# A perceiver block with routed experts on one core: one load moved up the queue, one projection moved between scores, second expert layers moved behind the next first half

## The chip, the cores and the metric

The kernel runs on one core of one Trainium2 chip. A core has TensorE (PE, matrix products; its weight loads are shown apart as PEld), VectorE (DVE), ScalarE (ACT), GpSimd (POOL) and SyncE (SP, which here only issues DMAs), each with its own in-order list of instructions. The metric is the device time of one execution in microseconds (us), as a median over runs. Everything is computed in float32.

## What is computed

The reference, cut to what matters. `x` is 64 sequences of 32 tokens of 256; `ctx_512` is 64 contexts of 257 rows of 128.

```python
x = x + xattn(layernorm(x), ctx_512)   # 16 heads of 64; q from x, k and v from the context; softmax over 257 rows
x = x + attn(layernorm(x))             # 4 heads of 64 over the 32 tokens of a sequence, half of each head rotated
x = x + ffn(layernorm(x))              # mixture of 8 experts, each token to its best 2

# ffn, for all 2048 tokens
scores = x @ Wr.T + br
idx    = top_k(scores + biases_N, 2);  val = softmax(scores) at idx, scaled to sum 1
h      = x @ Wl1[n] + bl1[n]           # 256 -> 1024, split in halves a and b
y      = sum over the two experts n of val[n] * ((silu(a) * b) @ Wl2[n] + bl2[n])   # 512 -> 256
```

## The kernel before

**Tiles and sequences.** The 2048 tokens are 16 tiles `t` of 128 tokens, that is 4 sequences `b` each. One loop over the 64 pairs (t, b) does the cross attention of a sequence and, between its pieces, other tiles' work. Two sequences overlap: while (t, b) is transposed and mixed, the scores of the next pair are made. `cross_probs` (L359) is a generator of four pieces: a score product `s` (L369), its negated maximum `nmx` on DVE (L373), the exponential `pr` on ACT with its sum (L374), and after each second one the scaling on DVE (L379, L381). The `s` tiles have three PSUM banks, so the fourth score of a sequence needs the bank of the first, which ACT's exponential frees. `probs_transposed` (L389) transposes the probabilities (`tp`, L392), `cross_mix` (L399) multiplies them with the context (`pa`, L402).

**What is done in between.** `work` holds three generators: "near" and "far" are `rest(t)` (L597) of the last finished tile and of the one before it, and "ahead" makes queries of later tiles. `rest` is `cross_output` (output projection `po`, L431 and L435), `self_attention` (transposes `trs`; the projection `pqkv`, L450, 2 products of 512 and 2 of 256 columns; `trqk`; scores `pss`; `pot`; output `apo`) and `route` (transposes `trr`, scores `pr`, ranks `pk`, two scatters of the rows to `routed` in memory, L578, then `pw` and `pb`). Each `next` does one piece. Which piece comes where is written by hand: the table `steps` has a row for each b of six places, and `step()` (L945) takes the next. Even and odd tiles use the same four rows. The row for b == 3 is

```python
        ("near", "far", "ahead", "", "far", "far"),
```

whose first "near" is the tile's `pqkv` group, standing ahead of the first two scores of the next pair. In odd tiles "ahead" is at its end by then.

**The 257th context row.** The loop treats 256 context rows; the last row's part is added as one product in `cross_output`, `po` <- `u`, `lastT` (L431), before the others of `po` (L435, four, a yield, four). The rows `u` are worked out once at the start, kept in memory (`u_last`), and `load_last(t)` (L296) fetches a tile's 64 rows with four DMAs into one of three buffers, at b == 3 of the tile.

**The experts.** Tokens are gathered from `routed` in blocks of 128 rows for one expert. Six early blocks are taken from what the tiles before the last three have scattered, so that they can run among the last tiles' remains; 28 late blocks follow, with branches for more that this input doesn't take. A block has five steps, all on `Blocks` (L660 on): `gathered` (one DMA, its row number read into a register of SP), `prepared` (transposes `pxT`, copy `bxT` on ACT, gate and target rows on DVE), `first_half` (`pa`, 8 groups of a pair of products, L726), `second_half` (`pb` the same; then `silu` of `pa` on ACT, L740, and `g` = (`pb` + bias) * silu on DVE, L745, four each), and `combined` (the second layer `py` <- `g`, L757; `y` = `py` * gate on DVE, L762; an accumulating scatter to the output by POOL, L763). Weights lie in lanes, three for the late blocks and two of them for the early ones; a lane holds both layers of an expert (1028 and 512 KB) and `weights` (L683) reloads a layer once its last reader is done, and only where the expert changes.

**Queues.** SP issues its DMAs in the program's order, and each waits for its buffer, so what stands behind a waiting one waits too. The order on PE and SP is the program's; on DVE, ACT and POOL a planner sets it from the program.

**Around the change.** In the last tile (t == 15) at b == 2, SP gets the six early gathers and the weights of block 0; at b == 3 comes `load_last(15)`. The gathered rows have five buffers, one of which was taken before, and the sixth gather needs the first block's to be free again. After the loop `do(...)` (L994) runs a hand-written list of units: "near" and "far" as above, and "x", "a", "b", "c" with a block's number for `prepared`, `first_half`, `second_half` and `combined`. Then `run` (L1027) does the late blocks:

```python
            blocks.first_half(b)
            blocks.second_half(b)
            if b + LANES < hi:
                blocks.weights(b + LANES, (0,))
            if b > lo:
                blocks.combined(b - 1)
```

Of the kernel before, what the change touches and what calls it, by code (L numbers as in the profile page):

```python
# [19 lines left out]
NT = TOK // P  # L20
# [16 lines left out]
EARLY = 6  # L37
LATE = NBK - EARLY
LANES = 3
LIKELY = (34 - EARLY, 36 - EARLY)  # L40
# [10 lines left out]
def block_kernel(  # L51
# [46 lines left out]
    def load(dst, src):  # L98
        nc.sync.dma_start(out=dst, in_=src)
# [16 lines left out]
    def load_tokens(t):  # L116
        xs[t] = xrp.tile([P, D], FP, tag="x", name=f"x{t}")
        load(xs[t], x[t * P : (t + 1) * P, :])

    def load_context(t):  # L120
        kv = kvp.tile([P, W1LEN], FP, tag="kv", name=f"kv{t}")
        kvT = kv[:, : 4 * M].rearrange("p (b m) -> p b m", b=4)
        kvA = kv[:, 4 * M : 4 * M + 4 * ML].rearrange("p (b c d) -> p b c d", b=4, c=MC)
        load(kvT, ctx_t[:, 4 * t : 4 * t + 4, :])
        load(kvA, ctx_a[:, 4 * t : 4 * t + 4, :, :])
        return kvT, kvA
# [54 lines left out]
    def iota(shape, pattern, base, by_partition, name):  # L181
        it = const.tile([P] + shape, FP, name=name)
        nc.gpsimd.iota(
            it,
            pattern,
            base=base,
            channel_multiplier=by_partition,
            allow_small_or_imprecise_dtypes=True,
        )
        return it  # L190
# [4 lines left out]
    before = iota([P], [[1, P]], 0, -1, "before")  # L195
# [7 lines left out]
    late = iota([LATE], [[1, LATE]], 0, 0, "late")  # L203
# [92 lines left out]
    def load_last(t):  # L296
        for h4 in range(4):
            load(
                u_ring[t % 3][h4 * 32 : h4 * 32 + 16, :],
                u_last[h4, 16 * t : 16 * t + 16, :],  # L300
            )
# [87 lines left out]
    def probs_transposed(t, b, j, pr, pts):  # L389
        tp = ps.tile([P, 4 * P], FP, tag="t", bufs=2, name=f"tp{t}_{b}_{j}")  # L390
        for g in range(4):
            nc.tensor.transpose(  # L392
                tp[:, g * P : (g + 1) * P], pr[:, g, j * P : (j + 1) * P], ident
            )
        pt = ptp.tile([P, 4 * P], FP, tag=f"pt{j}", name=f"pt{t}_{b}_{j}")
        nc.scalar.copy(pt, tp)  # L396
        pts.append(pt)
# [251 lines left out]
    def lane_of_queries(i):  # L649
        flat = qp.tile([P, 8, XH, SEQ], FP, tag="q", name=f"lane{i}")  # L650
        flat = flat.rearrange("p a h n -> p (a h n)")
        lanes.append((flat[:, :W1LEN], flat[:, W1LEN : W1LEN + W2LEN]))
# [118 lines left out]
    def early_blocks():  # L771


        bl = Blocks("early", EARLY, lambda b: b % 2)
        count = counted("early")
        full = in_blocks(count, 0, "early")
        last = up_to(full, "early")
        wide = [P, EARLY, NE]
        blk = early.rearrange("p a (l o) -> p (a l) o", o=1)
        past, eb = over_blocks(  # L780
            ALU.is_ge, blk.to_broadcast(wide), last.to_broadcast(wide), "eb_early"
        )
        _, begin = over_blocks(ALU.mult, past, full.to_broadcast(wide), "begin_early")
        nc.vector.tensor_tensor(bl.mine, early_expert, eb.to_broadcast(wide), ALU.is_equal)
        first = small([EARLY], "first_early")
        nc.vector.tensor_tensor(first, blk[:, :, 0], begin[:, :, 0], ALU.subtract)
        nc.vector.tensor_scalar(first, first, float(P), None, ALU.mult)
        ebf = eb[:, :, 0]
        nc.vector.scalar_tensor_tensor(
            bl.meta[:, 0, :], ebf, float(CAP), first, ALU.mult, ALU.add  # L790
        )
        nc.vector.tensor_copy(bl.meta[:, 1, :], ebf)
        nc.vector.tensor_tensor(bl.meta[:, 2, 2:], ebf[:, 2:], ebf[:, :-2], ALU.not_equal)
        done = small([1, NE], "done")
        nc.vector.tensor_tensor(done, full, last, ALU.subtract)
        nc.vector.tensor_scalar(done, done, float(EARLY), 0.0, ALU.add, ALU.max)
        nc.vector.tensor_tensor(done, done, full, ALU.min)
        return bl, done

    def late_blocks(done):  # L800
# [74 lines left out]
    steps = (  # L875
        ("", "far", "ahead", "near", "far", ""),
        ("near", "far", "", "near", "far", ""),
        ("ahead", "far", "ahead", "near", "far", "ahead"),
        ("near", "far", "ahead", "", "far", "far"),
    )  # L880
    kvs, probs = {0: context0}, {}
    seqs = [(t, b) for t in range(NT) for b in range(4)]
# [3 lines left out]
    with tc.tile_pool(name="rope", bufs=1) as rp:  # L886
# [27 lines left out]
        c4 = rp.tile([P, 16], FP, name="c4")  # L914
# [3 lines left out]
        c2 = rp.tile([P, 16], FP, name="c2")  # L918
# [12 lines left out]
    for n, (t, b) in enumerate(seqs):  # L931
        if t == NT - 1 and b == 0:
            blocks, done = early_blocks()
            lane_of_queries(0)
        if b == 0:
            cT = wk.tile([P, XH, 4, SEQ], FP, tag="cT", name=f"cT{t}")
            lastT = wk.tile([P, 4, SEQ], FP, tag="lastT", name=f"lastT{t}")
            if t + 1 < NT:
                kvs[t + 1] = load_context(t + 1)
            if t % 2 == 0 and t + 4 < NT:  # L940
                for j in (t + 4, t + 5):
                    load_tokens(j)
        place = iter(steps[b])

        def step():  # L945
            name = next(place)
            if name:
                next(work[name], None)

        scores = iter(())  # L950
        if n + 1 < len(seqs):
            t1, b1 = seqs[n + 1]
            scores = cross_probs(t1, b1, kvs[t1][0])
        pr, pts = probs.pop((t, b)), []
        probs_transposed(t, b, 0, pr, pts)
        step()
        next(scores, None)
        next(scores, None)
        step()
        probs_transposed(t, b, 1, pr, pts)  # L960
        nc.vector.transpose(lastT[:, b, :], p_last[t % 2][b])
        next(scores, None)
        step()
        next(scores, None)
        step()
        step()
        cross_mix(t, b, pts, kvs[t][1], cT)
        step()
        if t == NT - 1 and b == 2:
            for i in range(EARLY):  # L970
                blocks.gathered(i)
            blocks.weights(0, (0, 1), sure=True)
        if b == 3:
            load_last(t)
            if t % 2:
                for _ in work["ahead"]:
                    pass
                if t + 3 < NT:
                    work["ahead"] = cross_queries((t + 3) // 2)
                    next(work["ahead"])  # L980
            for _ in work["far"]:
                pass
            work["far"] = work["near"]
            work["near"] = rest(t, cT, lastT, u_ring[t % 3])
# [9 lines left out]
    def do(units):  # L994
        for unit in units.split():
            if unit in work:
                next(work[unit], None)
            else:
                b = int(unit[1:])
                {  # L1000
                    "x": blocks.prepared,
                    "a": blocks.first_half,
                    "b": blocks.second_half,
                    "c": blocks.combined,
                }[unit[0]](b)
                if unit[0] == "c" and b + 2 < EARLY:
                    blocks.weights(b + 2, (0, 1))

    do("near far x0")
    blocks.gathered(EARLY - 1)  # L1010
    do("near far near a0 far near b0 near far x1 c0 near a1 near far x2 b1 far a2")
    do("near c1 near far x3 b2 far near c2 far near a3 near x4 b3")
    late, total = late_blocks(done)
    do("c3")
    for b in range(3):
        late.gathered(b)
    do("near a4 near b4 x5 c4")
    late.weights(1, (0, 1))
    do("a5 b5")
    late.prepared(0)  # L1020
    do("c5")
    late.weights(2, (0, 1))
    blocks = late

    def run(lo, hi):  # L1027
        for b in range(lo, hi):
            if b + 3 < hi:
                blocks.gathered(b + 3)  # L1030
            if b + 1 < hi:
                blocks.prepared(b + 1)
            blocks.first_half(b)
            blocks.second_half(b)
            if b + LANES < hi:
                blocks.weights(b + LANES, (0,))
            if b > lo:
                blocks.combined(b - 1)
                if b - 1 + LANES < hi:
                    blocks.weights(b - 1 + LANES, (1,))  # L1040
            if b == 4:
                yield
        blocks.combined(hi - 1)
# [8 lines left out]

    main = run(0, LIKELY[0])
    next(main)
    used = nc.values_load(  # L1057
        total[0:1, :],
# [63 lines left out]
```

## Time and profile before

| | us |
|---|---|
| median of 3 runs | 852.11 (851.6 to 853.08) |
| the profiled execution, whole | 853.89 |
| its span, first to last instruction | 851.9 |
| TensorE granted clock, mean | 0.986 |
| first wait of TensorE, at the start | 7.27 |
| the 256 exponentials on ACT, L374 | 120.8 |
| the 512 score products, L369 | 143.4 |
| the 256 mixes, L402 | 123.3 |
| POOL's 28 late scatters, L763 | 43.4 |

The profile is of one execution. A row of a timeline gives its start, its length, the engine, the line and operation, what it writes and reads, how many instructions it merges, and in brackets how long the engine was idle before it and what ended that wait. A wait view sums such idle times: total, times, longest. "SPq" rows are SP issuing a DMA; their length is the time to issue, not the transfer. "PEclk" is the clock granted to TensorE, in tenths of full speed or as a mean.

### The profile page before, as it was taken

To read this page: it belongs to the slowest core of one execution; us is meant where nothing else is said; L and a number is where in the kernel's file an instruction comes from. 1 tells how busy PE (TensorE), PEld (TensorE's weight loads), DVE (VectorE), ACT (ScalarE), POOL (GpSimd) and SP (SyncE) were. 2 spreads that over 40 slices of the span, in tenths; PEclk is the share of its full clock that TensorE was granted. 3 is DMA by queue.
4 is the path that set the end of the run, shared out by engine and by line. 5 is a ranking of instruction groups with operands and counts; after the bars stand their busy time and mean duration, and the time that the engine had idled before them with its cause. 6 is when DMAs were issued, how large, how long until landed. Compare 5 with 4: busy or idle time off the path is not lost. (4 is left out here: it accounts for less than half of the span.)

```text
span 851.9 us, 15173 instructions
## 1 busy us (share of the span) xinstructions
PE 794.0 (93%) x5240; PEld 611.9 (72%) x5240; DVE 489.2 (57%) x2006; ACT 382.3 (45%) x1082; POOL 147.4 (17%) x209
## 2 busy tenths in 40 slices
PE   4899999999999999999999999999949999999994
PEld 3567677677767766776766777666647799999993
DVE  2456656766676676667676666767626733333331
ACT  2565545455455445546554545554414332222220
POOL 5001011111101011121101011110112422322222
PEclk9999999999999999999999999999979999999997
DMA  8421102020120202021120202012061297357321
GB/s 300 125 53 53 63 1 72 1 85 19 55 75 11 74 0 86 7 67 37 49 72 2 72 1 72 20 53 55 1 258 13 69 318 216 47 110 221 52 38 22
DMA packets 32031, 62.71 MB, mean 74 GB/s; under 512 B 5256, under 2 KB 22672, under 8 KB 30416
## 3 DMA queue, kind: packets, MB, share of 16 engines
q1 hardware_dynamic: 25424, 52.65, 19.0%
q0 software_dynamic: 6528, 9.06, 6.0%
q8 instruction: 43, 0.70, 0.3%
q14 instruction: 36, 0.29, 0.1%
HBM read 83.23 MB, written 13.16 MB: 113 GB/s over the span
## 5 line engine op out<-in xcount | busy, mean ns | idle before, releaser
L374 ACT ACTIVATE pr<-s,nmx 128x257 f32<-128x257 f32 x256 | 120.8, 479 | 72.6 <-DVE nmx L373 71.4
L369 PE MATMUL s<-kv,q 128*128 128x257 f32 x512 | 143.4, 389 | 7.6 <-ACT pr L374 7.6
L373 DVE TENSOR_REDUCE nmx<-s 128x1 f32<-128x257 f32 x256 | 103.8, 420 | 61.7 <-PE s L369 59.9
L402 PE MATMUL pa<-pt,kv 128*128 128x512 f32 x256 | 123.3, 604 | 5.0 <-ACT ov L426 5.0
L369 PEld LDWEIGHTS s<-kv,q 128*128 128x128 f32 x512 | 88.8, 192 | 25.1 <-ACT pr L374 12.2
L396 ACT COPY pt<-tp 128x512 f32<-128x512 f32 x128 | 75.9, 593 | 65.2 <-PE tp L392 65.1
L392 PEld LDWEIGHTS tp<-ident,pr 128*128 128x128 f32 x512 | 60.7, 144 | 33.7 <-issue 20.9
L392 PE MATMUL tp<-ident,pr 128*128 128x128 f32 x512 | 81.4, 280 | 1.2 <-DVE pr L381 1.1
L381 DVE TENSOR_SCALAR pr<-pr,inv 128x256 f32<-128x256 f32 x256 | 80.5, 357 | 2.9
L405 ACT COPY cT<-pa 128x512 f32<-128x512 f32 x64 | 37.5, 586 | 88.7 <-PE pa L402 88.7
L578 POOL DMA_INDIRECT routed<-xr,rslots x32 | 32.8, 1025 | 250.7 <-DVE pr L381 105.4
L402 PEld LDWEIGHTS pa<-pt,kv 128*128 128x128 f32 x256 | 44.9, 190 | 40.6 <-issue 29.1
L345 PE MATMUL pqh<-xqT,xwq_sb 128*128 128x256 f32 x256 | 62.5, 389 | 4.3 <-ACT xqT L253 4.3
L763 POOL DMA_INDIRECT out_x<-y_late,to_late x28 | 43.4, 1550 | 110.3 <-DVE gate_late L705 41.4
L435 PE MATMUL po<-xwo_sb,ov 128*128 128x256 f32 x256 | 61.9, 386 | 0.0
L345 PEld LDWEIGHTS pqh<-xqT,xwq_sb 128*128 128x128 f32 x256 | 48.6, 195 | 11.6 <-ACT xqT L253 4.7
L435 PEld LDWEIGHTS po<-xwo_sb,ov 128*128 128x128 f32 x256 | 49.7, 194 | 7.1
L379 DVE RECIPROCAL inv<-sums 128x2 f32<-128x2 f32 x128 | 20.6, 161 | 55.9 <-ACT pr L374 55.2
L745 DVE SCALAR_TENSOR_TENSOR g_late<-pb_late,lane,sa_late 128x128 f32<-128x128 f32 x72 | 20.3, 343 | 55.5 <-PE pb_late L726 37.0
L374 ACT ACTIVATION_READ_ACCUMULATOR pr<-s,nmx 128x1 f32 x256 | 51.8, 203 | 0.0
L410 POOL TENSOR_TENSOR xb<-x,xbo_bc 128x256 f32<-128x256 f32 x16 | 11.6, 725 | 213.7 <-issue 198.5
L450 PE MATMUL pqkv<-awqkv_sb,xaT 128*128 128x512 f32 (+1 forms) x128 | 43.9, 486 | 0.0
(256 smaller groups left out, 1286.5 us busy)
## 6 DMA issues: line engine op xcount, KB each, us to landing
lane<-in_wall SPq DMA_DIRECT2D x24, 1028.0 KB
lane<-in_wall SPq DMA_DIRECT2D x24, 512.0 KB
lane2a<-in_wall SPq DMA_DIRECT2D x10, 1028.0 KB
kv<-in_ctx_t SPq DMA_DIRECT2D x16, 514.0 KB
kv<-in_ctx_a SPq DMA_DIRECT2D x16, 512.0 KB
lane2b<-in_wall SPq DMA_DIRECT2D x10, 512.0 KB
xg_late<-routed SPq DMA_DIRECT2D x28, 132.5 KB
x<-in_x SPq DMA_DIRECT2D x16, 128.0 KB
```

Source lines behind the costliest of these rows:

```text
L345: nc.tensor.matmul(pq[:, mm, :], xwq_sb[:, k, m * P : (m + 1) * P], xqT[:, k, :], start=(k == 0), stop=(k == 1),)
L369: nc.tensor.matmul(s, qb[:, g * P : (g + 1) * P], kvT[:, b, :], start=True, stop=True)
L373: nc.vector.tensor_reduce(nmx, s, AX.X, ALU.max, negate=True)
L374: nc.scalar.activation(pr[:, g, :], s, AF.Exp, bias=nmx, accum_out=sums[:, g : g + 1])
L381: nc.vector.tensor_scalar(pr[:, i, :ML], pr[:, i, :ML], inv[:, i : i + 1], None, ALU.mult)
L392: nc.tensor.transpose(tp[:, g * P : (g + 1) * P], pr[:, g, j * P : (j + 1) * P], ident)
L396: nc.scalar.copy(pt, tp)
L402: nc.tensor.matmul(pa, kvA[:, b, j, :], pts[j], start=(j == 0), stop=(j == MC - 1))
L405: nc.scalar.copy(cT[:, :, b, :], pa.rearrange("p (h n) -> p h n", n=SEQ))
L435: nc.tensor.matmul(po, ov[:, m, :], xwo_sb[:, m, :], start=False, stop=(m == XH // 2 - 1))
L450: nc.tensor.matmul(pq, xaT[:, k, :], awqkv_sb[:, k, lo:hi], start=(k == 0), stop=(k == 1))
L763: nc.gpsimd.indirect_dma_start(out=out[:, :], out_offset=bass.IndirectOffsetOnAxis(ap=self.to[:, b : b + 1], axis=0), in_=y, in_offset=Non ...
```

## The change

Three edits.

1. `load_last(15)` is called at b == 2 of the last tile, ahead of the early gathers and the first weights, and no longer at b == 3 behind them.
2. `steps` has eight rows, four for even and four for odd tiles. The odd ones differ in the row for b == 3 alone: its first place is empty and "near", the `pqkv` group, is the third place, between the third and the fourth score of the next pair.
3. In the list after the loop and in `run`, the second layer of a block comes after the first half of the next block, not ahead of it or behind its second half; some "near", "far" and "x" units change places with their neighbours. The last early block's second layer and the load of the weights of late block 2 move into `run`, behind the first half of late block 0 (`last_early`).

```diff
@@ steps
         ("near", "far", "ahead", "", "far", "far"),
+        ("", "far", "ahead", "near", "far", ""),
+        ("near", "far", "", "near", "far", ""),
+        ("ahead", "far", "ahead", "near", "far", "ahead"),
+        ("", "far", "near", "", "far", "far"),
     )
...
-        place = iter(steps[b])
+        place = iter(steps[4 * (t % 2) + b])
...
         if t == NT - 1 and b == 2:
+            load_last(t)
             for i in range(EARLY):
                 blocks.gathered(i)
             blocks.weights(0, (0, 1), sure=True)
         if b == 3:
-            load_last(t)
+            if t < NT - 1:
+                load_last(t)
...
     do("near far x0")
     blocks.gathered(EARLY - 1)
-    do("near far near a0 far near b0 near far x1 c0 near a1 near far x2 b1 far a2")
-    do("near c1 near far x3 b2 far near c2 far near a3 near x4 b3")
+    do("near far near a0 far x1 b0 near far near c0 near a1 near far b1 x2 far a2 near c1")
+    do("far near x3 b2 far near c2 far near a3 near x4 b3")
     late, total = late_blocks(done)
-    do("c3")
+    do("a4 c3")
     for b in range(3):
         late.gathered(b)
-    do("near a4 near b4 x5 c4")
+    do("near b4 near x5 a5 c4")
     late.weights(1, (0, 1))
-    do("a5 b5")
+    do("b5")
     late.prepared(0)
-    do("c5")
-    late.weights(2, (0, 1))
-    blocks = late
+    early_ones, blocks = blocks, late
 
-    def run(lo, hi):
+    def run(lo, hi, before=None):
         for b in range(lo, hi):
             if b + 3 < hi:
                 blocks.gathered(b + 3)
             if b + 1 < hi:
                 blocks.prepared(b + 1)
             blocks.first_half(b)
-            blocks.second_half(b)
-            if b + LANES < hi:
-                blocks.weights(b + LANES, (0,))
             if b > lo:
                 blocks.combined(b - 1)
                 if b - 1 + LANES < hi:
                     blocks.weights(b - 1 + LANES, (1,))
+            elif before:
+                before()
+            blocks.second_half(b)
+            if b + LANES < hi:
+                blocks.weights(b + LANES, (0,))
...
+    def last_early():
+        early_ones.combined(EARLY - 1)
+        late.weights(2, (0, 1))
+
-    main = run(0, LIKELY[0])
+    main = run(0, LIKELY[0], last_early)
```

## The prediction

> **What bounds the kernel now.** I read the page first (busy shares, the 40 slices), then the chain, then TensorE's waits, then around its longest wait the timelines of PE, SP's queue and POOL, and last the end of the late blocks.
>
> ```profile
> PE 794.0 (93%) x5240; PEld 611.9 (72%) x5240; DVE 489.2 (57%) x2006; ACT 382.3 (45%) x1082; POOL 147.4 (17%) x209
> ...
> PEclk9999999999999999999999999999979999999997
> ```
> TensorE bounds nearly everything, so only its idle time (58 us of 851.9) and its slow slice, the 31st, can be won.
>
> ```profile
> PE po L431 <- DMA u<-u_last: 9.7, 1, 9.7
> PE s L369 <- ACT pr L374: 7.6, 10, 1.1
> ...
> PE py_early L757 <- DVE g_early L745: 2.1, 3, 0.9
> ...
> PE trs L252 <- DVE to_early L707: 1.3, 1, 1.3
> ```
> These are the waits that the three parts of the change touch. The timelines place them: PE, SP's queue, POOL, in that order.
>
> ```profile
> 546.33 0.70 PE L369 MATMUL s<-kv,q 128*128 128x257 f32 x2 [0.76 <-ACT pr L374]
> ...
> 617.11 0.38 PE L698 MATMUL pxT_early<-ident,xg_early 128*128 128x128 f32 x2
> 627.23 1.19 PE L431 MATMUL po<-u,lastT 128*128 128x256 f32 x2 [9.74 <-DMA u<-u_last]
> 628.22 3.22 PE L435 MATMUL po<-xwo_sb,ov 128*128 128x256 f32 x8
> ```
> ```profile
> 588.33 29.54 SPq L680 DMA_DIRECT2D xg_early<-routed  x6
> 618.44 0.87 SPq L689 DMA_DIRECT2D lane<-in_wall  x2
> 619.36 0.43 SPq L595 DMA_DIRECT2D out_x<-x  x1
> 619.83 2.08 SPq L99 DMA_DIRECT2D u<-u_last  x4
> 621.96 0.65 SPq L99 DMA_DIRECT2D lane2a<-in_wall  x1
> 624.40 0.36 SPq L99 DMA_DIRECT2D lane2b<-in_wall  x1
> ```
> The sixth gather holds SP until x0's transposes (617.11) free its buffer. Behind it stand the first weights, and behind these the four u loads; so TensorE, ready at 617.49, stood until 627.23.
>
> ```profile
> 627.23 0.96 POOL L578 DMA_INDIRECT routed<-xr,rslots  x1 [5.61 <-DMA routed<-xr,rslots]
> 634.29 0.72 POOL L520 TENSOR_TENSOR axb<-x,abo_bc 128x256 f32<-128x256 f32 x1 [6.10 <-DVE x L440]
> 636.24 0.57 POOL L242 TENSOR_TENSOR rstds<-ves,minus_half 128x1 f32<-128x1 f32 x1 [1.23 <-DVE ves L240]
> ```
> POOL's second scatter of tile 13 waits for the first; tile 15's rstds stands behind it. It was covered by the stall.
>
> ```profile
> 769.97 1.12 DVE L745 SCALAR_TENSOR_TENSOR g_late<-pb_late,lane2a,sa_late 128x128 f32<-128x128 f32 x4 [3.08 <-PE pb_late L726]
> ...
> 843.16 1.55 POOL L763 DMA_INDIRECT out_x<-y_late,to_late  x1 [3.18 <-DMA out_x<-y_late,to_late]
> ```
> The late blocks run without a TensorE wait. The end hangs on the second last scatter's DMA, not on the last product.
>
> **What the skill says.** (1) "TensorE: Matmul & The Clock Gate", Part 1: an idle window of some 3.4 us halves the clock, a busy one restores it. The trace agrees: the windows view grants 0.50 from 622 to 627.2, 0.51 to 631, 1.00 after. (2) "DMA: Bandwidth & Descriptors", Anatomy of one DMA: 2.0 us plus bytes at 436 GB/s, an estimate of 4.4 us for 1028 KB. Here it was longer: lane2b's issue waited 1.7 us "<- DMA lane" until 624.35, so I read the first weights (issued 618.44) as landed then, 5.9 us. I use 5.9. (3) Same page, Issuing engines are not separate DMA queues: all run on the same 16 engines; 622 to 627.2 shows them 94% busy, so fetching u sooner does not make the weights land much sooner. (4) The first page, "Architectural detail: the array is 16× 32×32, not 1× 128×128": ACT, DVE and each GpSimd core are strict FIFO, as rstds behind the scatter shows.
>
> **Part 1, u sooner.** Its four issues (4 x about 0.46 us on SP) now stand before the gathers of 588.33, in a gap of SP (583.40+1.84 to 588.33, 3.1 us); the gathered rows are first used at 617. Free. Removed: 9.74 us of wait and the slow clock after it: L431 and the first half of L435 took 631.37-627.23=4.14 us here (the next row, pss, starts at 631.37) and 593.32-591.16=2.16 for tile 14, so 2.0. Together 11.7.
> What is late next? I count u from 617.49. TensorE now does po 2.16, pss 0.31, po's rest 1.73: at u=4.2 it wants pa_early of block 0. Its weights still follow x0 on SP and land at 624.35, u=6.9. New wait 2.6 us (1.6 to 3.2: u's 64 KB lie no longer behind it, lane2's 1540 KB come sooner). A pause this long may drop the clock once: 0 to 1.7 us (half of 3.4), I take 0.7.
> Then pa 1.79, pot 0.6, pxT 0.22, pb 1.79: u=11.3, and trs of tile 15 is due. POOL's second scatter still waits for the first one's DMA until 627.2 (u=9.7): 0.96 scatter, 0.72 axb, 0.57 rstds, 0.41 xns (DVE L245), 0.2 of hand-overs, u=12.6. New wait 1.3, in place of the old 1.30 there (0 to 2).
> Part 1 net: 11.7-2.6-0.7=8.4.
>
> **Part 2, the order up to the first late blocks.** The products are the same. Old waits in that stretch besides those above: pxT 0.77, apo 0.93, g_early 0.93+0.93+0.28, together 3.8; they go because a first half now stands ahead of each second layer (1.79 us of cover for g's 1.13) and pxT stands after pb. New ones, from the order of the changed build and the rows of before:
> - trqk of tile 15: DVE now does apo's sum, bn, xr (2.5 us) ahead of the qkv sums and rotation (2.3 us): late by 0.5.
> - pa_early of block 2: in before bxT's copy ended 650.82-645.26=5.56 us after the first half of block 1 began, behind an activation-table load of 1.28 and apr. TensorE now wants it after 1.79+0.31+0.22+1.79+0.22+0.37=4.7: late by 0.8.
> - pot then waits for diag: 0.4.
> - trr of tile 15: POOL now has a scatter (1.18) ahead of rstdr, itself behind y_early's (1.58): late by 1.3.
> - pa_early of block 5 stands right after its own pxT: copy 0.37 and two hand-overs, 0.5.
> - py_early of block 4: g's last three are strewn through DVE's chain of late_blocks, which takes 678.18-668.36=9.8 us in before; late by 0.9. No g stands between metadata and gathers more than before.
> - pa_late of block 0 after its pxT: 0.3.
> Sum 4.7 against 3.8: -0.9 (bounds +3 and -4, as each rests on a list in order of mean durations). The first late weights keep 1.3 us of cover (issue to landing 5.3 us read off the DMA traffic of 680 to 686).
>
> **Part 3, odd tiles.** In t=1, 3 .. 13 the fourth score waits for ACT: 0.84+6x0.76=5.4 us, since nothing stands between third and fourth. The two pqkv groups (2.58 us) now do. Checks: s0 starts 2.6 us sooner, its bank was free long before; the qkv sums then end 2.6+0.5 us later, 4 us ahead of trqk; pa needs pqkv's bank, which DVE frees about 0.6 us before; the next tp needs the fourth softmax's scaling, which ends within 0.2 us of need. I take 5.0 (3.3 to 5.4). Even tiles keep their rows; tile 15 has no scores left there.
>
> **Part 4, late blocks.** py(b-1) now follows pxT and pa(b), 0.22+1.79=2.01 us after pb(b-1). g starts 0.1 us after pb and takes 1.12: ready after 1.28 with a hand-over. Slack 0.73 in each block, no wait. y(b-1) (0.48) runs under pb(b). SP's two weight waits change places with what releases them. In the middle it is worth 0.
> At the end: y of block 26 comes 1.79 us sooner, so its scatter does (838.43 to 836.65) and its DMA, 843.16-838.43=4.73 later, at 841.38. The last py now waits 1.26 for its g: py ends 840.8, y 841.3, scatter 841.55. Against 843.16: 1.6 gained (0 to 1.8).
>
> **Sum.** 8.4-0.9+5.0+1.6=14.1 of 851.9: span 837.8. That execution took 853.89 whole, 1.99 around the span, so 839.8 for it; it lies 1.8 above the median of 852.11. On the median: 838.0.
>
> **Rivals.**
> - More cover (12%): weights land by u=4.2 and none of the new waits of part 2 arises: 11.7+3.8+1.3+5.4+1.6=23.8, 828. For it: each of them is my list, not a row. Against: weights and scatter are DMAs that no edit moves.
> - The stall moves (19%): clock falls, the weights come at u=7.4, part 2 loses its 4, part 3 gives 3.3: 11.7-3.2-1.7-4+3.3+0.5=6.6, 845.5. For it: the DMA engines are full from 619 to 634. It covers the case that the change brings only half of what it says.
> - No change within 0.2% (2%): pa_early waits as long as po did. Against: weights landed 2.9 us before u, and po's products come ahead.
> - Slower (4%): g not ready in the late blocks. Decides from 0.73 us beyond my 1.28; each us more costs 27, so 0.52 us of wait per block eats the 14.1 and 1 us gives 865. For it: 0.73 us is thin, and the slack is the same in all blocks, so a miss would be paid 27 times. Against: g's start 0.1 us after pb and its 1.12 us recur in every block of before, and DVE is busy 40.8 of 118 us from 720 to 838.
>
> **Numbers.** Likeliest case 63%, 832 to 843. Range 830 to 846 (the first two rivals partly left out). This kernel's measurement can tell about 0.2%, 1.7 us: faster 94%, within 2%, slower 4%.
>
> **What would show it.** Right: no PE wait on u; one of 2 to 3 us at pa_early on lane and about 1 us at trs; no s<-ACT wait of 0.76 in odd tiles; py_late with no wait but the last, about 1.2; the last scatter some 3.7 us after the last pb ends. Wrong: a py_late wait in every block, a pa_early wait over 4 us, or a clock of 0.5 for more than 4 us after 615.

## The result and the profile after

| | before | changed |
|---|---|---|
| median of 4 runs each, us | 851.86 (850.83 to 853.08) | 836.32 (835.06 to 837.68) |
| ratio | | 0.9818 [0.9804, 0.9831] |
| profiled execution, whole, us | 853.89 | 835.06 |
| its span, us | 851.9 | 833.3 |

The changed kernel takes 15.5 us less (14.4 to 16.7 by the interval). I had forecast 838.0, 14.1 less. Run again beside another series of before it took 836.74 against 851.85, ratio 0.9822 [0.9797, 0.9846].

The page of the changed kernel, TensorE's busy time and its granted clock by slices:

```profile
PE 792.6 (95%) x5240; PEld 613.0 (74%) x5240; DVE 490.1 (59%) x2006; ACT 378.5 (45%) x1080; POOL 147.2 (18%) x209
...
PEclk9999999999999999999999999999999999999998
```

TensorE is as busy as before to 1.4 us; the slow slice is gone (it is the 30th of the 40, not the 31st, as the prediction has it). So what was won is idle time and the slow clock behind it. The waits of TensorE in the changed kernel (engine, line, what it waited for, then total, times, longest in us):

```profile
PE tp L392 <- DVE pr L381: 2.0, 3, 0.8
PE pa_early L726 <- DMA lane<-in_wall: 1.9, 1, 1.9
PE s L369 <- ACT pr L374: 1.8, 2, 1.1
...
PE pa_early L726 <- ACT bxT_early L700: 1.0, 2, 0.5
...
PE trs L252 <- DVE xns L245: 0.7, 1, 0.7
PE py_late L757 <- DVE g_late L745: 0.5, 1, 0.5
PE trqk L252 <- DVE qkv L465: 0.4, 1, 0.4
PE pxT_late L698 <- DVE g_early L745: 0.4, 1, 0.4
```

No wait on `u` is left. Its place is taken by the first weights (1.9); `trs` still waits 0.7. `s` fell from 10 waits to 2, `py_early` has none, `py_late` one of 28. The timeline of PE in the same kernel shows the places:

```profile
536.70 0.60 PE L369 MATMUL s<-kv,q 128*128 128x257 f32 x2
537.14 2.74 PE L450 MATMUL pqkv<-awqkv_sb,xaT 128*128 128x512 f32 x8
539.72 0.60 PE L369 MATMUL s<-kv,q 128*128 128x257 f32 x2
...
610.11 0.38 PE L698 MATMUL pxT_early<-ident,xg_early 128*128 128x128 f32 x2
610.37 0.70 PE L431 MATMUL po<-u,lastT 128*128 128x256 f32 x2
...
616.95 2.98 PE L726 MATMUL pa_early<-bxT_early,lane 128*128 128x128 f32 x16 [1.92 <-DMA lane<-in_wall]
619.87 1.12 PE L509 MATMUL pot<-diag,qkv 128*64 128x128 f32 x8
...
623.96 0.44 PE L252 MATMUL trs<-ident,xns 128*128 128x128 f32 x2 [0.67 <-DVE xns L245]
...
645.50 0.44 PE L252 MATMUL trr<-ident,xr 128*128 128x128 f32 x2 [1.40 <-DVE xr L245]
...
821.56 1.99 PE L757 MATMUL py_late<-lane2b,g_late 128*128 128x256 f32 x8 [0.50 <-DVE g_late L745]
```

In tile 13 the projection stands between the third and the fourth score, and the fourth no longer waits. `po` on `u` follows `x0`'s transposes at once. SP's queue of the changed kernel (the length of a merged row includes the waits between its issues):

```profile
576.96 4.70 SPq L99 DMA_DIRECT2D u<-u_last  x8
582.48 28.38 SPq L680 DMA_DIRECT2D xg_early<-routed  x6
611.43 0.87 SPq L689 DMA_DIRECT2D lane<-in_wall  x2
```

The last `u` load is issued by 581.7, nearly 30 us before it is used. The sixth gather still holds SP until `x0` has read its buffer, and the weights stand behind it as before. POOL in the changed kernel, around `trs` and at the end:

```profile
613.30 1.06 POOL L578 DMA_INDIRECT routed<-xr,rslots  x1 [17.00 <-DMA xg_early<-routed]
621.22 0.96 POOL L578 DMA_INDIRECT routed<-xr,rslots  x1 [6.85 <-DMA routed<-xr,rslots]
622.20 0.74 POOL L520 TENSOR_TENSOR axb<-x,abo_bc 128x256 f32<-128x256 f32 x1
622.88 0.57 POOL L242 TENSOR_TENSOR rstds<-ves,minus_half 128x1 f32<-128x1 f32 x1
...
824.53 1.55 POOL L763 DMA_INDIRECT out_x<-y_late,to_late  x1 [2.90 <-DVE y_late L762]
```

In this execution the last scatter waits for its own `y`, no longer for the DMA of the scatter before it.

The first of these rows shows a second thing that the gather holds. The first scatter of tile 13 writes `routed`, which the early gathers read. Its row numbers were ready at 602.84, yet it started at 613.30, when the sixth gather had landed. The second scatter waits for the first, and tile 15's `rstds`, on which `trs` hangs, stands behind both: its input was ready at 618.04, and it started at 622.88.

**One part of the difference is not the change's.** The spans differ by 18.6 us. Near the start, where both programs are the same, one execution lost the clock and the other didn't. The same stretch of the windows view, before:

```profile
33.80:37.00 3.20, 3.20 (x11) 2.63 (x12) 0.88 (x3) 1.84 (x6) 0.00 (x0) 0.50 0.03 8
```

and changed:

```profile
33.80:37.00 3.20, 3.20 (x24) 2.91 (x23) 2.29 (x7) 2.89 (x10) 0.00 (x0) 1.00 0.01 3
```

The third number from the right is the granted clock: 0.50 against 1.00. The product after it, `pv` (L263), starts at 38.03 and at 36.19, so 1.84 us come from the start of the program, not from the change. The slow clock at this place is in three of the twelve profiles of this study. 16.8 us are left, at the upper edge of the interval of the medians (14.4 to 16.7): the stamps are of one pair of executions, of which the changed one is the fastest of its four. Three stamps split them. `trs` of tile 15 starts at 623.96 in the changed kernel; in the kernel before it is

```profile
637.40 0.41 PE L252 MATMUL trs<-ident,xns 128*128 128x128 f32 x2 [1.30 <-DVE to_early L707]
```

and the third `pxT_late` starts at 688.63 before and at 672.12 changed.

| stretch | before, us | changed, us | gained, us | forecast, us |
|---|---|---|---|---|
| start to `x0`'s transposes, less the 1.84 | 617.11 | 610.11 | 5.16 | 5.0 (part 3) |
| from there to `trs` of tile 15, the 2.0 of block 0's `pb` and block 1's `pxT`, now ahead of it, taken off | 20.29 | 13.85-2.0 | 8.4 | 8.4 (part 1) |
| from `trs` to the third `pxT_late`, the 2.0 given back | 51.23 | 48.16+2.0 | 1.1 | -0.9 (part 2) |
| from there to the last scatter | 154.53 | 152.41 | 2.1 | 1.6 (part 4) |
| sum | | | 16.8 | 14.1 |

### The profile page after: what moved, and what is told of

It reads as the page before. It is cut to its first block, busy times and chain, and to the rows that moved or that the text cites. A ratio compares the mean times of both kernels' runs of the same rounds, so it can differ in the third digit from the quotient of the medians.

```text
span 833.3 us, 15141 instructions
## 1 busy us (share of the span) xinstructions
PE 792.6 (95%) x5240; PEld 613.0 (74%) x5240; DVE 490.1 (59%) x2006; ACT 378.5 (45%) x1080; POOL 147.2 (18%) x209
## 5 line engine op out<-in xcount | busy, mean ns | idle before, releaser
L369 PE MATMUL s<-kv,q 128*128 128x257 f32 x512 | 141.3, 385 | 1.8 <-ACT pr L374 1.8
L762 DVE TENSOR_SCALAR y_late<-py_late,gate_late 128x256 f32<-128x256 f32 x28 | 13.6, 484 | 62.0 <-PE py_late L757 62.0
```

The lines of the kernel that those rows point to most:

```text
L369: nc.tensor.matmul(s, qb[:, g * P : (g + 1) * P], kvT[:, b, :], start=True, stop=True)
```

## The experiments

Each was timed in five rounds against runs of the kernel before on the same chip. Differences are of medians.

**1. Each edit alone.** First the load alone, edit 1 in the kernel before:

```diff
         if t == NT - 1 and b == 2:
+            load_last(t)
             for i in range(EARLY):
...
         if b == 3:
-            load_last(t)
+            if t < NT - 1:
+                load_last(t)
```

> The kernel before with edit 1 alone (the last tile's u rows fetched ahead of the gathers). Theory A (the stall is handed on): PE no longer waits for u, but pa_early of block 0 waits about 1.9 us for its weights with a slow clock after it (some 1.8 us), and trs of tile 15, which in this order comes ahead of pb, waits some 3 us for POOL's scatter instead of 1.3; net about 6 us less than before. Theory B (the sum of the prediction's part 1): 8.4 us less. Theory C (nothing is late next): 11.7 us less.

Measured: 846.43 against 852.95, ratio 0.993 [0.9914, 0.9946], so 6.5 us, less than the 8.4 that the same part is worth inside the whole change. Its timeline of PE says why:

```profile
621.53 2.05 PE L726 MATMUL pa_early<-bxT_early,lane 128*128 128x128 f32 x16 [1.83 <-DMA lane<-in_wall]
623.52 0.66 PE L509 MATMUL pot<-diag,qkv 128*64 128x128 f32 x8
628.28 0.51 PE L252 MATMUL trs<-ident,xns 128*128 128x128 f32 x2 [4.11 <-DVE xns L245]
628.59 3.52 PE L726 MATMUL pb_early<-bxT_early,lane 128*128 128x128 f32 x16
```

The wait for the weights is the same (1.83 against 1.92), but in the old order nothing stands between `pot` and `trs`. TensorE meets the end of POOL's chain 4.1 us early and loses the clock on top (`pb` takes 3.52 instead of 1.95). In the whole change, block 1's `pxT` and block 0's `pb` stand there. By these rows the order is what makes part 1 worth its 8.4.

Then the rows of odd tiles alone, edit 2:

```diff
-        place = iter(steps[b])
+        place = iter(steps[4 * (t % 2) + b])
```

> The kernel before with edit 2 alone (odd tiles' rows). Theory A: six of the seven waits of 0.76 us go whole, the first tile's 0.84 turns into a wait of tp for pr; 4.6 us less than before. Theory B: all seven go, 5.4 us less. Theory C: the 18.6 us between the two spans held a larger share of this edit, 7.0 us less, as the stamp of x0's transposes (617.11 against 610.11) reads at first sight; then the stamps up to tile 1 must differ for a reason in the kernel and not by the clock at the start.

Measured: 848.29 against 852.95, ratio 0.995 [0.9936, 0.9965], 4.7 us. The waits of `s` on `pr` fell to 2.1 us in 3.

Then the order alone, edit 3, the list after the loop and the late blocks as in the change, the other two edits left out:

> The kernel before with edit 3 alone (order of the list after the loop and of the late blocks). The wait for u of 9.7 us stays. Theory A: old waits of 3.8 us and trs's 1.3 go, new ones of about 3.2 us come (trqk, two for bxT, trr, pxT_late), and the end gains 2.1; net about 4 us less than before. Theory B (the prediction's sum for parts 2 and 4): 0.7 us less. Theory C: the late order alone, 2.1 us less.

Measured: 849.67 against 852.95, ratio 0.9966 [0.995, 0.9982], 3.3 us (1.5 to 4.3). Its eight runs lie in two groups, 847.1 to 848.7 and 850.7 to 851.1, and the median falls between them. A gain of 0.7 is excluded, but theory B was not all that the prediction says of this edit: `trs`'s wait of 1.3 is covered here by the new order and is gone from the trace, and the prediction had counted that in part 1. With it, its sums give -0.9+1.6+1.3=2.0, which lies inside the interval, as do theories A and C. So this run doesn't decide about part 2. The three edits alone add to 14.5, the whole gives 15.5; they all but add up.

**2. Where does the wait for the weights come from?** The row that holds SP is the sixth gather. It is issued once at b == 2 and a second time after the loop (`blocks.gathered(EARLY - 1)`), so the first can go, and nothing of what is computed is left out. In the kernel before, alone:

```diff
         if t == NT - 1 and b == 2:
-            for i in range(EARLY):
+            for i in range(EARLY - 1):
                 blocks.gathered(i)
```

> The kernel before with one change that is not in the change under study: only five early gathers at b == 2, the sixth is made once, later, where both kernels make it a second time. Theory A (SP's queue behind the sixth gather is the cause): weights of block 0 and u are both there before they are wanted, tile 13's scatters no longer share the DMA engines with the weights; no wait for u or for weights, 11 to 13 us less than before. Theory B (the transfers themselves are late): about as edit 1 alone, 6 us.

Measured: 842.18 against 852.95, ratio 0.9884 [0.9867, 0.99], 10.8 us: one edit of one line gives more than the load moved up. SP's queue of this kernel:

```profile
586.02 3.79 SPq L680 DMA_DIRECT2D xg_early<-routed  x5
590.73 0.90 SPq L689 DMA_DIRECT2D lane<-in_wall  x2
613.25 0.35 SPq L595 DMA_DIRECT2D out_x<-x  x1
613.65 1.81 SPq L99 DMA_DIRECT2D u<-u_last  x4
```

and its PE:

```profile
616.81 0.67 PE L431 MATMUL po<-u,lastT 128*128 128x256 f32 x2 [1.22 <-DMA u<-u_last]
...
621.28 1.95 PE L726 MATMUL pa_early<-bxT_early,lane 128*128 128x128 f32 x16
```

The weights go out at 590.73 and are there when they are wanted. `u`, still at its old place, is behind the store of tile 13's rows and comes 1.2 us late. TensorE's wait is 8.5 us shorter, and the 2.0 of slow clock behind it are gone, together 10.5 of the 10.8. So the stall of 9.74 us in the kernel before was the gather's doing; the `u` load was only the row at which it showed.

The same line in the changed kernel:

> The changed kernel with the early sixth gather left out as well. Theory A (SP's queue is what hands the stall on to the weights): the wait of 1.9 us of pa_early for its weights goes, the slow clock after it (pa_early 2.92 us from start to start of the next row, 1.79 at full clock) too, and trs's 0.7; some 4 us less than the changed kernel, 19.5 less than before. Theory B (the weights' own transfer is too long): the changed kernel's 15.5 less than before, no more.

Measured: 831.97 against 853.32, ratio 0.9745 [0.9726, 0.9764], 21.4 us, some 4 to 6 more than the change, which wasn't in this series. Neither the wait for the weights nor the one of `trs` is in its trace; its PE:

```profile
614.18 1.95 PE L726 MATMUL pa_early<-bxT_early,lane 128*128 128x128 f32 x16
...
618.75 0.38 PE L252 MATMUL trs<-ident,xns 128*128 128x128 f32 x2
```

and its POOL:

```profile
602.94 1.06 POOL L578 DMA_INDIRECT routed<-xr,rslots  x1 [7.33 <-issue]
```

Tile 13's first scatter starts 0.8 us after its row numbers are ready, not 10.5, and its second at 605.80, long before `rstds`. So the wait for `u` in the kernel before, and in the changed one the wait for the weights and the late POOL chain in front of `trs`, had one cause, the sixth gather: SP's queue hands its wait to what stands behind it, and `routed`, which it reads, hands it to the scatters.

**3. The late order.** The changed kernel with the loop of `run` in its old order:

```diff
             blocks.first_half(b)
-            if b > lo:
-                blocks.combined(b - 1)
-                if b - 1 + LANES < hi:
-                    blocks.weights(b - 1 + LANES, (1,))
-            elif before:
+            if b == lo and before:
                 before()
             blocks.second_half(b)
             if b + LANES < hi:
                 blocks.weights(b + LANES, (0,))
+            if b > lo:
+                blocks.combined(b - 1)
+                if b - 1 + LANES < hi:
+                    blocks.weights(b - 1 + LANES, (1,))
```

> The changed kernel with the old order in the late blocks (both halves, then the second layer of the block before), all else as changed. Theory A (the new late order pays at the end alone): no py_late wait, the second last scatter's DMA bounds the end again, the last scatter starts some 4.7 us after the one before it; 2 us more than the changed kernel, 13.5 less than before. Theory B (the late order is worth nothing or costs): 15.5 less than before or more.

Measured: 837.58 against 853.32, ratio 0.9815 [0.9797, 0.9834]. As the changed kernel wasn't in that series, both went once more, side by side:

> The changed kernel itself, beside the next run on one chip, since the profile of the late blocks in the old order shows its last scatter 2.1 us later after the first pxT_late while its time was the changed kernel's within the interval. Both theories: 15.5 us less than before (14.4 to 16.7).

> The changed kernel with the late blocks in the old order, again. Theory A (the end gains what the stamps show): 1.5 to 2.5 us more than the run before it. Theory B (the time lies elsewhere at the end, the stamps don't carry over): within 0.8 us of it.

Measured: 836.74 for the changed kernel, 836.53 with the old late order (ratios 0.9822 [0.9797, 0.9846] and 0.9819 [0.9795, 0.9842] against 851.85). In stamps, from the first `pxT_late` to the last scatter, the six profiles with the old order took 160.8 to 161.4 us. Of the six with the new order, five took 158.7 to 159.7, and one, of the changed kernel without the early sixth gather, 161.7. The scatters say why the gain comes and goes. With the old order the last one waits for the DMA of the one before it in all six; with the new one it waits for its own `y` in four, and in two for the one before it again, as in the second profile of the changed kernel:

```profile
825.03 1.55 POOL L763 DMA_INDIRECT out_x<-y_late,to_late  x1 [3.12 <-DMA out_x<-y_late,to_late]
```

There the last scatters follow each other 4.5 to 4.7 us apart, and 6.0 to 6.4 in the profile that took 161.7, so a `y` that is ready sooner wins less or nothing. The stamps mostly show 1.1 to 2.7 us, and the time doesn't. A gain of 1 to 2 us is not excluded by intervals of that width, but it isn't shown either, and stays open. Nor is a loss shown: none of 27 blocks waits for its `g`.

**4. What is left of the list.** On top of the changed kernel without the early sixth gather: tile 14 with the odd rows as well, block 2's `pxT` ahead of a "near", a "far" and block 1's second half, block 5's `pxT` ahead of block 4's second half and a "near", so that each copy of `bxT` has a product beside it.

```diff
-        place = iter(steps[4 * (t % 2) + b])
+        place = iter(steps[4 * (t % 2 or t == NT - 2) + b])
...
-    do("near far near a0 far x1 b0 near far near c0 near a1 near far b1 x2 far a2 near c1")
+    do("near far near a0 far x1 b0 near far near c0 near a1 x2 near far b1 far a2 near c1")
...
-    do("near b4 near x5 a5 c4")
+    do("near x5 b4 near a5 c4")
```

> The changed kernel without the early sixth gather, with the odd rows for tile 14 too, and with pxT of early blocks 2 and 5 moved one or two places ahead. On top of that run without the sixth gather: theory A: the s<-ACT wait of tile 14 (0.76 us) and the two waits of pa_early for bxT (0.49 and 0.52) go, 1.8 us less; theory B: DVE or ACT are late at the next place instead, under 0.5 us less.

Measured: 830.87 against 853.32, ratio 0.9745 [0.9723, 0.9767], 1.1 less than that kernel. Both `bxT` waits and tile 14's wait of 0.76 for `pr` are gone from its trace, and a wait of 0.9 of `pot` on `diag` is new. The times don't tell a gain from none.

And then tile 15's `apo` ahead of tile 14's `pk`, so that `rstdr` comes before the scatter on POOL:

```diff
-    do("far near x3 b2 far near c2 far near a3 near x4 b3")
+    do("near far x3 b2 far near c2 far near a3 near x4 b3")
```

> The kernel of the run above with apo of tile 15 ahead of pk of tile 14, so that POOL makes tile 15's rstdr ahead of tile 14's first scatter. Theory A (the scatter on POOL holds rstdr and so trr): trr's wait of 1.4 us falls to a few tenths, apo may wait some 0.5 us for oT; about 0.9 us less than the run above. Theory B (trr waits for DVE's own chain): no change, or apo's wait eats it.

Measured: 829.29 against 853.32, ratio 0.9732 [0.9709, 0.9756], 24.0 us, the fastest kernel of the study, faster than both kernels of the change. Its POOL:

```profile
639.09 0.57 POOL L242 TENSOR_TENSOR rstdr<-ver,minus_half 128x1 f32<-128x1 f32 x1 [0.43 <-DVE rslots L576]
639.87 1.17 POOL L578 DMA_INDIRECT routed<-xr,rslots  x1 [0.21 <-POOL rstdr L242]
```

In the changed kernel it was the other way round (scatter 643.37, `rstdr` 644.40), and tile 15's `trr` stood 1.40 us for it; that wait is gone here. The 1.6 us between the last two kernels lie within their intervals.

## Why the prediction was right, step by step

The time lies 1.7 us below the forecast. The stamps lie 2.7 us beyond it: 2.0 in part 2, whose sign was wrong, 0.5 in part 4 and 0.2 in part 3. Part 1 fits to 0.1 us, but by two errors that cancel. So the size owes something to luck; what was right is the main mechanism, a stall that goes and is handed on in part to the weights.

**Part 1, forecast 8.4, by stamps 8.4.** The `u` wait and the slow clock behind it went whole. The weights ended a wait of 1.92, in my 1.6 to 3.2 but below my 2.6: they landed about 5.5 us after issue (611.43 to 616.95), not 5.9. The 5.9 was read off the trace; the fit that the prediction quotes beside it from the Trainium skill ("DMA: Bandwidth & Descriptors", Anatomy of one DMA), 4.4 us, stands there for DMAs issued from GpSimd, and these loads are issued by SP. The second scatter stood behind the first one's DMA as said, about 1 us later than I took (621.22 is u = 10.7, forecast 9.7). That `rstds` waits its turn on POOL I had read off the kernel before, whose row doesn't show it (`rstds` waited 1.23 us for DVE there); the changed kernel does, where it starts 4.8 us after its input. Why the scatters were late, the sixth gather, the prediction doesn't have.

One term of the sum was wrong in kind: the clock. I had put it at 0.7 beside a wait of 1.3 at `trs`. It fell whole: `pa` 2.98 instead of 1.95, `pot` 1.12 instead of 0.66, block 1's `pxT` 0.59 instead of 0.44, in all 1.6. But the two don't add. `trs` waits for POOL's chain, so what the slow clock takes, the wait gives back. The kernel with the old late order has the same work in this stretch, and in its second profile the clock held; its PE:

```profile
616.55 2.05 PE L726 MATMUL pa_early<-bxT_early,lane 128*128 128x128 f32 x16 [1.81 <-DMA lane<-in_wall]
618.53 0.66 PE L509 MATMUL pot<-diag,qkv 128*64 128x128 f32 x8
...
623.23 0.44 PE L252 MATMUL trs<-ident,xns 128*128 128x128 f32 x2 [1.88 <-DVE xns L245]
```

The products are fast here and `trs` waits 1.88 instead of 0.67. From `x0` to `trs` it is 13.85 and 13.35 us in the two profiles with the fall, 13.41 and 13.25 in the two without. The 0.7 was counted twice; the later scatter made up for it, so the part came out right by luck, by two small errors of opposite sign.

**Part 2, forecast -0.9, by stamps +1.1.** The step that failed is my list of new waits, 4.7 us. It measured 3.2: `trqk` 0.42 (0.5), `pa_early` of block 2 0.49 (0.8), `trr` 1.40 (1.3), `pa_early` of block 5 0.52 (0.5), the late `pxT` 0.36 (0.3) came; `pot` on `diag` (0.4) and `py_early` of block 4 on a strewn `g` (0.9) are in no wait view of this kernel. Both were argued from DVE's order with mean durations, the weakest reasons of the list. The old waits of 3.8 went as said. Of the 2.0 us between forecast and stamps these waits explain 1.5; the other 0.5 stays open. The stamp repeats: from `trs` to the first `pxT_late` it is 44.9 us in the three profiles of the old order with a full clock there, and 41.6 to 41.9 in six of the new one, with 2.0 to be given back. The time of the order alone (1.5 to 4.3) doesn't confirm it: with `trs`'s 1.3 the forecast gives 2.0 there, and the stamps 1.1+2.1+1.3=4.5, just outside.

**Part 3, forecast 5.0, by stamps 5.2 and alone 4.7.** The wait went in six of seven odd tiles. In tile 1 its 0.84 turned into 0.83 us of `tp` waiting for the scaling of `pr`, the place that I had within 0.2 us of need.

**Part 4, forecast 1.6, by stamps 2.1, in time not shown.** In the middle nothing waits, so the slower rival (g not ready, 4%) is refuted by 27 blocks. That the end hangs on `y` and not on the scatter before it came true in one of the two profiles of the changed kernel, and in four of the six with the new order; the forecast had the two within 0.1 us of each other (841.3 and 841.38). At the end `py` waited 0.50, not my 1.26: DVE makes `g` in four pieces from 821.16, and `py` starts at 821.56, after the first (0.34 us), not after all four. The last scatter stands 3.5 us behind the last `pb`, forecast 3.7.

**The rivals.** More cover (828) asked for the weights by u = 4.2; they came at 6.5. Only when the duplicate gather was dropped did this half of it come about, at 831.97; the new waits of part 2 were still there (3.4 us in that trace). The moved stall (845.5) had its clock fall, but the fall lay in front of a wait and cost nothing that the stamps show. I missed the best edit though I had shown its row: the row of the gathers that keeps SP for 29.54 us stands in my lines of its queue, and I took it as given because no edit moved it.

## What to carry to other kernels

When a transfer ends a wait, go up its queue to the instruction that held it before moving the transfer: here the held gather was worth 10.8 us by one line, moving the load out of its way 6.5. Ask also what else hangs on the held instruction: here the scatters that write what it reads waited too, on another engine. Two waits in a row don't add when the second is on a chain that doesn't depend on the first; work out when each chain ends and take the later end. An edit can take away the cover of another wait (here `trs` waits 4.11 us with the load alone and 0.67 in the whole change), so look at such edits together as well as alone; the times alone, 14.5 in parts against 15.5, hardly tell it.

## What the runs showed of the hardware

The length of a wait does not by itself decide whether the clock falls. At the same place of the same stretch, waits of TensorE of 1.79, 1.81 and 1.83 us left the clock at 1.00, and waits of 1.92 and 2.12 us cost it. Near the start, idle times of 1.06, 0.78 and 0.36 us within 3 us are followed by 0.50 in the kernel before (33.8 to 37.0), and the same three, to the hundredth, by 1.00 in the kernel with the odd rows alone. The windows view of the changed kernel around the wait of 1.92:

```profile
616.00:618.50 2.50, 1.55 (x11) 1.55 (x12) 1.90 (x8) 0.00 (x0) 0.00 (x0) 0.87 1.03 391
618.50:620.00 1.50, 1.50 (x9) 1.28 (x10) 0.00 (x0) 0.00 (x0) 0.00 (x0) 0.50 1.03 429
```

The clock falls when the products have been running again for about 1 us (0.86 for 617.5 to 618 and 0.50 after), and is back at 621.3, so it is low for about 3.4 us. The Trainium skill ("TensorE: Matmul & The Clock Gate", Part 1) gives a free-running window of 3413 ns, which agrees with that length. It tells of an idle window of that length as the cause; here an idle time of 1.9 us was enough. Since the page's window runs free of the program, equal waits could fall differently in it, which would fit both places; no run here tests it.
